# Last image's z by channel chunk, each chunk normalized in one operation per tile and written for all images while the next chunk is made

## Chip, cores, metric

One core of one Trainium2 chip. The time is the device time of that core in microseconds (us), the median of several executions; lower is better.

## What is computed

Eight images of 512 channels and 32 x 32 positions, fp32, pass two layers. The first is attention with 8 heads and a residual. The second is a non-local block whose last steps matter here:

```python
f_div_C = einsum('bcn,bdn->bcd', theta_x, phi_x) / n
y = einsum('bcd,bdn->bcn', f_div_C, g_x)
z = conv1x1(y, W_w, W_b) + x
mean = z.mean(axis=(0, 2, 3)); var = z.var(axis=(0, 2, 3))      # over all images
out = (z - mean) * rsqrt(var + 1e-5) * gamma + beta
```

Mean and variance run over all images and positions of a channel. So no output of a channel can be written before z of the *last* image is known for that channel, but different channels don't wait for each other.

## The kernel before

Channels lie on 128 partitions in four chunks (`CC` = 4). z of images 0 to 5 is spilled to HBM, images 6 and 7 stay in SBUF (`KEEP` = 2). During the last image, images 0 to 2 are reloaded into buffers that fall free early; 3 to 5 follow at the end. `mats` holds the large matrices, `ring` has twelve blocks of 128x1024, and a pool's tag sets which tiles share a buffer.

```python
    # nonlocal_, for every image (cut): f from theta and phi, g, then wf = f * W
        nc.scalar.copy(wf, ps)
        ...                                  # eight sums on VectorE for the seven-product form
        seven(f"pz_{b}", Blocks(), data, False, first_z, add_to(xt))     # x += wf * g, all chunks
        for oc in range(CC):
            for h in range(NH):
                nc.vector.bn_stats(stats[:, oc, b * NH + h, :], xt[:, oc, h * 512:(h + 1) * 512])
            ...                              # spill of images 0 to 5
    # after the last image
    reload(3, "o")                           # buffer of theta and phi of the last image
    for b in range(4, B - KEEP):
        reload_chunks(b)                     # images 4 and 5, into ring blocks
    ...                                      # a soundness count is loaded into registers
    for cc in range(CC):
        nc.vector.bn_aggr(mv[:, cc, :], stats[:, cc, :, :].rearrange("p s k -> p (s k)"))
    ...                                      # gs = gamma / sqrt(var + eps) for all chunks
    for b in sorted(z, reverse=True):
        for cc in range(CC):
            t = z[b][cc]
            nc.vector.tensor_scalar(t, t, mv[:, cc, 0:1], gs[:, cc:cc + 1], ALU.subtract, ALU.mult)
            nc.scalar.activation(t, t, AF.Identity, bias=beta[:, cc:cc + 1])
            nc.sync.dma_start(out_v[b, :, cc, :], t)
```

`seven` is a seven-product (Strassen-like) form of a 2x2 block matrix product. All transfers named here are issued by SP (SyncE).

## Time and profile before

| | before |
|---|---|
| time, median of the first 3 runs | 2346.35 us (2342.19 to 2347.3) |
| span of the profiled run, granted clock | 2342.2 us, 0.982 |
| TensorE busy | 2240.7 us, 96% |
| gap between last reads and first writes | 11.2 us |
| writes of the output | 41.6 us at 402 GB/s |

Two terms of the profile: the *share* is the mean busy share of the core's 16 DMA engines, which do the transfers, and the *granted clock* is the part of full speed that TensorE's clock ran at.

The profile is read from the end of the span backwards, because only the end is touched: first the slices, then windows of the last 70 us, then the timeline. Those lines stand in the prediction. One more line is needed as a mark. The copy of f on ScalarE ends the part that the change does not reach; its timeline line in the kernel before is

```profile
2269.23 0.60 ACT L361 ACTIVATE f<-pf 128x512 f32<-128x512 f32 x1 [11.37 <-PE pf L359]
```

(columns: start in us, duration, engine, line, operation, output<-input, shapes, count, and in brackets the engine's idle time before it and who ended it). **f to end** below means the span's end less the start of this line: 2342.2 - 2269.23 = 73.0 us here. It is the measure of most experiments, because the 2270 us before f vary from run to run.

### The profile page before, as it was taken

Reading aid. Unit: us, or ns where it says so; the run is one execution under the profiler, and the core shown is the slowest. Engines: PE = TensorE matmul, PEld = TensorE weight load, DVE = VectorE, ACT = ScalarE, POOL = GpSimd, SP = SyncE. Lnnn points to the kernel's source line nnn. Section 1 sums busy time; section 2 is a strip of 40 time slices with the busy share of each in tenths; the row PEclk is TensorE's granted clock in tenths of the full one; section 3 lists DMA queues with packets and bytes.
Section 4 is the critical chain, followed back from the end, with each engine's and each line's share of the span. In section 5 each row is a group of like instructions: output and inputs, shape, how many; then the busy total and the mean of one; then the engine's idle time right before and its main releaser. Section 6 shows DMA issues by size and latency. Waiting matters only on the chain.

```text
span 2342.2 us, 20797 instructions
## 1 busy us (share of the span) xinstructions
PE 2240.7 (96%) x8562; PEld 1127.6 (48%) x8562; DVE 1397.7 (60%) x1261; ACT 704.4 (30%) x819; POOL 61.7 (3%) x56
## 2 busy tenths in 40 slices
PE   4999999999999999999999999999999999999990
PEld 1533655336643466434563355633655346643360
DVE  2277445783567744687348854488445773477745
ACT  0155102541035310453104521154202541035205
POOL 2000110000000000000000000000000000000000
PEclk7999999999999999999999999999999999999995
DMA  6000122001130021200121002210113001200327
GB/s 233 1 1 7 64 85 108 28 1 63 47 135 1 1 76 66 104 1 32 48 94 72 1 32 76 90 48 1 63 47 135 1 1 63 79 16 1 108 86 310
DMA packets 30950, 141.94 MB, mean 61 GB/s; under 512 B 4096, under 2 KB 10496, under 8 KB 26112
## 3 DMA queue, kind: packets, MB, share of 16 engines
q1 hardware_dynamic: 26000, 131.87, 15.2%
q10 hardware_dynamic: 4848, 8.67, 1.0%
q8 instruction: 69, 1.13, 0.2%
q14 instruction: 33, 0.27, 0.0%
HBM read 101.07 MB, written 39.45 MB: 60 GB/s over the span
## 4 chain that ended last, share of the span: by engine, by line
PE 94%; ACT 2%; DVE 1%; DMA 1%; POOL 0%; issue 0%; ACTq 0%; DVEq 0%; POOLq 0%
PE ps L270 20%; PE po L289 17%; PE pv L171 8%; PE ptp L171 8%; PE pk L171 8%; PE pp L171 8%; PE pq L171 8%; PE pg L171 4%; PE pz L171 4%; PE pf L359 2%; PE psum L289 1%; PE pwf L378 1%; ACT z L504 1%; PE po L287 1%; PE po L286 1%; PE psum L287 1%
## 5 line engine op out<-in xcount | busy, mean ns | idle before, releaser
L273 ACT ACTIVATE e<-ps 128x1024 f32<-128x1024 f32 x512 | 482.5, 1030 | 360.3 <-PE ps L270 360.3
L279 DVE TENSOR_TENSOR acc<-acc,e 128x1024 f32<-128x1024 f32 x384 | 467.4, 1217 | 164.0 <-ACT e L273 135.7
L270 PE MATMUL ps<-q,k 64*128 64x512 f32 x2048 | 473.3, 603 | 1.6 <-POOL q L256 1.6
L289 PE MATMUL po<-e,v 128*64 128x512 f32 x1904 | 464.3, 594 | 0.0
L270 PEld LDWEIGHTS ps<-q,k 64*128 64x128 f32 x2048 | 187.6, 187 | 284.2 <-issue 233.6
L289 PEld LDWEIGHTS po<-e,v 128*64 128x64 f32 x1904 | 153.3, 137 | 211.9 <-issue 200.7
L297 DVE RECIPROCAL ri<-psum 128x512 f32<-128x512 f32 x64 | 214.5, 3352 | 10.2 <-PE psum L289 10.2
L368 ACT ACTIVATE g<-pg,gb 128x512 f32<-128x512 f32 x32 | 22.0, 687 | 428.6 <-PE pg L171 428.6
L171 PE MATMUL pq<-t_x,w_WqT 128*128 128x512 f32 x256 | 117.8, 608 | 26.0 <-ACT q L228 21.1
L188 DVE TENSOR_TENSOR k<-k,pk 128x1024 f32<-128x1024 f32 x24 | 29.3, 1221 | 163.1 <-PE pk L171 163.1
L171 PE MATMUL pp<-t_o,w_WpT 128*128 128x512 f32 x256 | 116.3, 602 | 1.9 <-DVE x L331 1.9
L171 PE MATMUL ptp<-w_tp,t_x 128*128 128x256 f32 x512 | 114.4, 379 | 0.0
L171 PE MATMUL pv<-w_WvT,t_x 128*128 128x256 f32 x512 | 114.4, 379 | 0.0
L171 PE MATMUL pk<-t_x,w_WkT 128*128 128x512 f32 x256 | 113.8, 592 | 0.0
L171 PEld LDWEIGHTS ptp<-w_tp,t_x 128*128 128x128 f32 x512 | 97.3, 190 | 13.2
L171 PEld LDWEIGHTS pv<-w_WvT,t_x 128*128 128x128 f32 x512 | 97.3, 190 | 13.2
L228 ACT ACTIVATE q<-pq,bq 128x512 f32<-128x512 f32 x64 | 40.4, 684 | 182.8 <-PE pq L171 182.8
L171 PE MATMUL pq<-x,w_WqT 128*128 128x512 f32 x192 | 88.7, 605 | 5.3 <-DMA w_WqT<-in_WqT_dram 5.3
L171 PEld LDWEIGHTS pq<-t_x,w_WqT 128*128 128x128 f32 x256 | 49.9, 196 | 90.1 <-issue 62.4
L188 DVE TENSOR_TENSOR q<-q,pq 128x1024 f32<-128x1024 f32 x24 | 29.3, 1221 | 102.1 <-PE pq L171 102.1
L277 DVE TENSOR_TENSOR acc<-e,e 128x1024 f32<-128x1024 f32 x64 | 78.3, 1223 | 16.6 <-ACT e L273 15.7
L171 PE MATMUL pp<-o,w_WpT 128*128 128x512 f32 x192 | 88.2, 603 | 0.0
(117 smaller groups left out, 2193.2 us busy)
## 6 DMA issues: line engine op xcount, KB each, us to landing
x<-in_x_dram SPq DMA_DIRECT2D x32, 512.0 KB, 5.5
w_WpT<-kept_WpT SPq DMA_DIRECT2D x7, 1792.0 KB, 7.1
w_tp<-kept_tp SPq DMA_DIRECT2D x7, 1792.0 KB, 7.2
spill<-x SPq DMA_DIRECT2D x24, 512.0 KB, 3.8
z<-spill SPq DMA_DIRECT2D x24, 512.0 KB, 8.4
out_dram<-z SPq DMA_DIRECT2D x24, 512.0 KB, 6.0
w_WqT<-kept_WqT SPq DMA_DIRECT2D x6, 1792.0 KB, 7.4
w_WvT<-kept_WvT SPq DMA_DIRECT2D x6, 1792.0 KB, 7.0
```

What stands on the lines that cost most here:

```text
L171: pe(nc.tensor.matmul(to_ps, lhsT(k), rhs(k), start=(s, at) not in begun, stop=(k == nk - 1), skip_group_check=True))
L188: nc.vector.tensor_tensor(at, at, ps, ALU.add)
L228: nc.scalar.activation(t[:, c, cols(q)], ps[:, m, :], AF.Identity, bias=bias[:, c:c + 1])
L270: pe(nc.tensor.matmul(ps[:, j, :], k[r, p, m * P:(m + 1) * P], q[r, p, h * 512:(h + 1) * 512], start=True, stop=True))
L273: nc.scalar.activation(e, ps, AF.Exp, scale=SCALE)
L277: nc.vector.tensor_tensor(accs[p, h], es[p, h, 0], e, ALU.add)
L279: nc.vector.tensor_tensor(accs[p, h], accs[p, h], e, ALU.add)
L286: pe(nc.tensor.matmul(to[:, :LEAD], l, r[:, :LEAD], start=start, stop=False, skip_group_check=True))
L287: pe(nc.tensor.matmul(to[:, LEAD:], l, r[:, LEAD:], start=False, stop=stop, skip_group_check=True))
L289: pe(nc.tensor.matmul(to, l, r, start=start, stop=stop, skip_group_check=True))
L297: nc.vector.reciprocal(ri, ps)
L359: pe(nc.tensor.matmul(ps[:, c, :], tp[:, i, c * P:(c + 1) * P], tp[:, i, CI:], start=(i == 0), stop=(i == NB - 1)))
```

## The change

Intent: start writing as soon as the first chunk of channels is done. For the last image z is made chunk by chunk with a plain product; each chunk is then aggregated, and each of its eight tiles (one per image) is normalized in *one* operation, `t * gs + (beta - mean * gs)`, alternately on VectorE and ScalarE, and written while TensorE and VectorE make the next chunk.

```diff
+        if before_z:
+            before_z()                       # reloads of images 3, 4, 5
+            last_z(b, xt, wf, g)
+            return
...
+    def last_z(b, xt, wf, g):
+        z[b] = [xt[:, oc, :] for oc in range(CC)]
+        for oc in range(CC):
+            ps = next_bank(f"pz_{b}_{oc}")
+            for h in range(NH):
+                s = slice(h * 512, (h + 1) * 512)
+                for d in range(IC):
+                    pe(nc.tensor.matmul(ps[:, h, :], wf[:, d, oc * P:(oc + 1) * P], g[d][:, s], ...))
+                nc.vector.scalar_tensor_tensor(xt[:, oc, s], ps[:, h, :], wb[:, oc:oc + 1], xt[:, oc, s],
+                                               ALU.add, ALU.add)
+                nc.vector.bn_stats(stats[:, oc, b * NH + h, :], xt[:, oc, s])
+            batch_norm(oc)
+
+    def batch_norm(oc):
+        nc.vector.bn_aggr(mv[:, oc, :], ...)
+        nc.scalar.activation(gs, mv[:, oc, 1:2], AF.Sqrt, bias=eps)
+        ...                                  # gs = gamma / that; shift = beta - mean * gs
+        for i, b in enumerate(sorted(z, reverse=True)):
+            t = z[b][oc]
+            if i % 2:
+                nc.scalar.activation(t, t, AF.Identity, bias=shift, scale=gs)
+            else:
+                nc.vector.tensor_scalar(t, t, gs, shift, ALU.mult, ALU.add)
+            nc.sync.dma_start(out_v[b, :, oc, :], t)
...
-    (the reloads after the last image, the aggregation of all chunks,
-     and the loop over images with two operations per tile)
```

More of the change, by code (lines that the diff above doesn't have):

```diff
@@ L212, in unshifted @@
         nc.vector.memset(heads[j * D:(j + 1) * D, j * D:(j + 1) * D], 1.0)
+    mv = const.tile([P, CC, 2], F32, tag="mv", name="mv")
     gates = const.tile([P, B * NPAIR], F32, tag="gates", name="gates")
@@ L349, in theta_phi, with nonlocal_ @@
         return tp
-    def nonlocal_(b, xt, data, tp, wg):
+    def nonlocal_(b, xt, data, tp, wg, before_z):
         g = [w2.tile([P, N], F32, tag="acc", name=f"g_{b}_{d}") for d in range(IC)]
@@ L373, in nonlocal_ @@
         wf = block(f"wf_{b}")
-        ws = block(f"ws_{b}")
         ps = next_bank(f"pwf_{b}")
@@ L380, in nonlocal_ @@
         nc.scalar.copy(wf, ps)
+        if before_z:
+            before_z()
+            last_z(b, xt, wf, g)
+            return
         half = C // 2
+        ws = block(f"ws_{b}")
         w = [wf[:, 0, :half], wf[:, 1, :half], wf[:, 1, half:]] + [ws[:, i, j * half:(j + 1) * half]
@@ L413, in nonlocal_ @@
                 nc.sync.dma_start(spill[b][:, oc, :], xt[:, oc, :])
+    def last_z(b, xt, wf, g):
[5 more added lines that the diff above has]
+                for d in range(IC):
+                    pe(nc.tensor.matmul(ps[:, h, :], wf[:, d, oc * P:(oc + 1) * P], g[d][:, s],
+                                        start=(d == 0), stop=(d == IC - 1)))
+                nc.vector.scalar_tensor_tensor(xt[:, oc, s], ps[:, h, :], wb[:, oc:oc + 1], xt[:, oc, s],
[3 more added lines that the diff above has]
+    def batch_norm(oc):
+        nc.vector.bn_aggr(mv[:, oc, :], stats[:, oc, :, :].rearrange("p s k -> p (s k)"))
+        gs, shift = (small.tile([P, 1], F32, tag=n, name=f"{n}_{oc}") for n in ("gs", "shift"))
+        nc.scalar.activation(gs, mv[:, oc, 1:2], AF.Sqrt, bias=eps)
+        nc.vector.reciprocal(gs, gs)
+        nc.vector.tensor_tensor(gs, gs, gamma[:, oc:oc + 1], ALU.mult)
+        nc.vector.tensor_tensor(shift, mv[:, oc, 0:1], gs, ALU.mult)
+        nc.vector.tensor_tensor(shift, beta[:, oc:oc + 1], shift, ALU.subtract)
+        for i, b in enumerate(sorted(z, reverse=True)):
[5 more added lines that the diff above has]
+            nc.sync.dma_start(out_v[b, :, oc, :], t)
     z = {}
@@ L428, in reload_chunks, with reload_rest @@
             z[b].append(t)
+    def reload_rest():
+        reload(3, "o")
+        for b in range(4, B - KEEP):
+            reload_chunks(b)
     data = data_sums(quarters_of(xt), "x_0")
@@ L470, in unshifted @@
             w["v"] = load_w("WvT", b + 2, nc.sync, None)
-        nonlocal_(b, xt, data, tp, w["g"])
+        nonlocal_(b, xt, data, tp, w["g"], reload_rest if last else None)
         if b < B - 2:
             w["k"] = load_w("WkT", b + 2, nc.sync, None)
-        if b >= B - KEEP:
+        if B - KEEP <= b < B - 1:
             z[b] = [xt[:, cc, :] for cc in range(CC)]
         xt = nxt.get("x")
-    reload(3, "o")
-    for b in range(4, B - KEEP):
-        reload_chunks(b)
     good = const.tile([P, 1], F32, tag="good", name="good")
@@ L488, in unshifted @@
     sound = nc.values_load(count, min_val=0, max_val=P)
-    mv = const.tile([P, CC, 2], F32, tag="mv", name="mv")
-    for cc in range(CC):
-        nc.vector.bn_aggr(mv[:, cc, :], stats[:, cc, :, :].rearrange("p s k -> p (s k)"))
-    rstd = const.tile([P, CC], F32, tag="rstd", name="rstd")
-    nc.scalar.activation(rstd, mv[:, :, 1], AF.Sqrt, bias=eps)
-    nc.vector.reciprocal(rstd, rstd)
-    gs = const.tile([P, CC], F32, tag="gs", name="gs")
-    nc.vector.tensor_tensor(gs, rstd, gamma, ALU.mult)
-    for b in sorted(z, reverse=True):
-        for cc in range(CC):
-            t = z[b][cc]
-            nc.vector.tensor_scalar(t, t, mv[:, cc, 0:1], gs[:, cc:cc + 1], ALU.subtract, ALU.mult)
-            nc.scalar.activation(t, t, AF.Identity, bias=beta[:, cc:cc + 1])
-            nc.sync.dma_start(out_v[b, :, cc, :], t)
     return sound
```

## The prediction

> **What bounds the kernel now.** Read first the page's rows by slices, then the chain, then the windows of the last 70 us, because the change touches only the last image's z and what follows it: with line numbers and buffer numbers taken off, the instruction order of both kernels is the same on every engine up to the product that makes the last z.
>
> ```profile
> PE   4999999999999999999999999999999999999990
> DMA  6000122001130021200121002210113001200327
> PE 94%; ACT 2%; DVE 1%; DMA 1%; POOL 0%; issue 0%; ACTq 0%; DVEq 0%; POOLq 0%
> ```
>
> TensorE is busy in all but the first and last slice of 58.6 us each, and the chain is 94% TensorE. So some 2275 of 2342 us are closed to this change. The last slice alone has an idle TensorE and a DMA row at 7. Cut finely, that end is three stretches and a rest (columns: stretch, length, busy time of PE, PEld, DVE, ACT, POOL, granted clock, DMA share, GB/s):
>
> ```profile
> 2270.40:2286.70 16.30, 15.14 (x36) 6.21 (x35) 10.21 (x16) 2.98 (x3) 0.00 (x0) 1.00 0.99 378
> 2286.90:2297.10 10.20, 1.20 (x5) 0.35 (x3) 9.77 (x19) 1.49 (x3) 0.00 (x0) 0.74 0.02 6
> 2298.00:2339.60 41.60, 0.00 (x0) 0.00 (x0) 20.29 (x29) 31.29 (x31) 0.00 (x0) 0.50 1.01 402
> 2339.70:2342.20 2.50, 0.00 (x0) 0.00 (x0) 0.00 (x0) 0.00 (x0) 0.00 (x0) 0.50 0.04 16
> ```
>
> First the transfers read spilled z back at a full DMA share (0.99). Then for some 11 us they do nothing (0.02) while VectorE finishes the last z, its statistics and the mean and variance. Then the 32 writes of the output run at share 1.01 and 402 GB/s until 2339.6. In that third stretch ScalarE is busy 31.3 of 41.6 us and VectorE 20.3, so neither holds the writes back: the end is set by the DMA engines. The chain view names ACT there ("ACT z L504"), since it follows instructions; it stops at 2329.3, 10 us before the last byte. The timeline around the gap:
>
> ```profile
> 2271.07 6.65 SPq L427 DMA_DIRECT2D z<-spill  x8
> ...
> 2275.50 1.98 PE L171 MATMUL pz<-g,wf 128*128 128x512 f32 x4 [1.16 <-ACT wf L380]
> ...
> 2292.38 1.91 DVE L493 BATCH_NORM_AGGREGATE mv<-stats 128x2 f32<-128x96 f32 x4
> ...
> 2295.06 5.87 DVE L503 TENSOR_SCALAR x<-x,mv,gs 128x1024 f32<-128x1024 f32 x8
> ...
> 2297.08 8.26 SPq L505 DMA_DIRECT2D out_dram<-x  x8
> ```
>
> The last z starts at 2275.5; the first write can go only after all four channel chunks have z, statistics and scale, at 2297.1. The reads ended at about 2286.8. The gap is 2298.0 - 2286.8 = **11.2 us**.
>
> **What the Trainium skill says.** (1) "DMA: Bandwidth & Descriptors", section "Queues, rings and completion order": on each DMA engine the descriptors of one ring are consumed in ring order. Reads and writes are all issued by SP, so early writes queue up behind the reads and don't overtake them. The trace agrees: the reloads at L427 took 7.8 to 10.9 us to land, where eight transfers of 1.3 us (0.524 MB at 402 GB/s) stand in line. (2) The same page, "Where 436 GB/s comes from", lets the HBM side bind at about 358 GB/s. The trace differs: 402 GB/s over 41.6 us of writes. I use 402. (3) "ScalarE: Activation LUTs", "What ACT_TABLE_LOAD costs": about 280 ns + 0.833 ns per element with one per-partition pointer operand, 93 ns more for each further one. The trace agrees for one: 280 + 853 = 1133 ns, and L504 has 1134. The new form takes bias and scale by pointer: an estimate from that section of 1.23 us. (4) "VectorE: DVE Perf Modes", "Mode 2×_2P": fp32 tensor_scalar from SBUF to SBUF may take two elements a cycle, tensor_tensor can't. The trace agrees: 0.82 us for L503 against 1.21 for L188 on the same 128x1024. The new tensor_scalar with two pointers is the same form as L503, so it stays fast.
>
> ```profile
> L504 ACT ACTIVATE z<-z,beta 128x1024 f32<-128x1024 f32 x24 | 25.1, 1134 | 0.0
> L503 DVE TENSOR_SCALAR z<-z,mv,gs 128x1024 f32<-128x1024 f32 x24 | 17.5, 825 | 0.0
> L404 DVE SCALAR_TENSOR_TENSOR x<-pz,Wb,x 128x512 f32<-128x512 f32 x8 | 5.6, 744 | 0.7 <-PE pz L171 0.7
> L411 DVE BATCH_NORM_STATS2 stats<-x 128x6 f32<-128x512 f32 x8 | 5.1, 680 | 0.0
> L493 DVE BATCH_NORM_AGGREGATE mv<-stats 128x2 f32<-128x96 f32 x4 | 1.9, 530 | 0.0
> ```
>
> **The change, part by part.** *The product.* The seven-product form is left for the last image: 14 matmuls become 16 plain ones. A matmul shows as two records 0.43 us apart, so 32 x 0.43 = 13.8 us in place of 28 x 0.43 = 12.0: 1.8 us more TensorE. A chunk is four matmuls, 3.4 us. It starts as before, when wf is copied (2275.5). Gone from VectorE are eight small sums for that form (4 x 0.69 + 4 x 0.42 = 4.4 us) and three additions of 1.21.
>
> *The first write.* TensorE gives the first half of chunk 0 at 2277.3 and the second at 2279.0. VectorE adds the second half to x (0.7, to 2279.8), takes its statistics (0.7, to 2280.5), aggregates (0.5, to 2281.0). ScalarE's square root takes 0.3, but in the compiled order VectorE puts an addition and statistics of chunk 1 in between (1.4, to 2282.4). Then the reciprocal (0.18) and three one-column operations of 0.16, with gaps 0.8, to 2283.2; one tensor_scalar, 0.8, to **2284.0**. Before, it was 2297.1: 13.1 us earlier. It is also 2.8 us before the reads end, so the DMA engines should not fall idle: before, data moved some 0.9 us after the first issue, which gives 2284.9 against 2286.8.
>
> *Feeding it.* A chunk is written for all 8 images: 8 x 0.524 MB = 4.19 MB, 10.4 us at 402 GB/s. VectorE needs per chunk 2 x 0.70 (add) + 2 x 0.61 (statistics, back to back) + 0.46 + 0.18 + 3 x 0.16 + 4 x 0.73 (the spacing in L503's 24) = 6.7 us; ScalarE 0.3 + 4 x 1.13 to 1.23 = 4.8 to 5.2; TensorE 3.4. All lie under 10.4, beside the writes. The halving of ScalarE's normalizing (32 activations to 16, some 16 us less) is worth nothing, as it lay under the writes already.
>
> *The end.* Bytes are the same: 12 reloads and 32 writes. The writes start where the reads end: 2286.8 + 41.6 = 2328.4, plus the 2.5 us after the last byte = 2330.9 in place of 2342.2. The gain is the gap, **11.2 us**. One thing moves to the end: the load of the soundness count and the branch on it came before the writes in SP's order and now come after them. Before, the last issue was at about 2336 and the last byte at 2339.6, so some 3 us hide it; I add 0.2. Predicted: 2346.35 - 11.2 + 0.2 = **2335.4 us**.
>
> **Rivals.** *A new wait holds the first writes.* In the compiled order VectorE's first chunk is x of image 7, then images 3, 5 and 1. Image 5's chunk 0 is the ninth of twelve reloads and lands at about 2284, just when it is wanted; the writes stand in SP's order, so one late tile stops all behind it. If the first burst slips by 4 us, 1 to 2 us of the gap come back: 2337. Against it: four tiles are ready by 2286, 5 us of traffic. *Reads and writes that meet slow each other.* They meet only at the border, with up to eight transfers in line. If the meeting cost a tenth for 10 us, 1 us: 2336. The windows of before, where they don't meet, say nothing on it. *VectorE becomes the bound.* It would take over 10.4 us per chunk in place of 6.7; with waits for PSUM and for the square root I find no more than 8. If it did at 12, the writes would end some 6 us later: 2341. *The better side:* if the 13.1 us by which the first write is earlier were gained whole, 2333. Against it: the DMA engines were already full until 2286.8. *ScalarE sets the end*, as the chain suggests: then the earlier start (13 us) and the halved activations (16 us) would both count, some 29 us, 2317. Against it: the share of 1.01 and the ten microseconds of transfers after its last activation.
>
> **Range and chances.** Three runs of before spread over 5 us (2342 to 2347), which is half the gain, and another chip may add as much. The rivals reach from 2333 to 2341. So 2330 to 2341 for 8 in 10. A gain of 2% would be 47 us; the whole end from 2275.5 has 66.7, of which 41.6 are writes at full share, so it can't be had. Slower by 2% would need the writes to run at half their rate. Chances: faster 0.01, within 2% 0.985, slower 0.005.
>
> **What would show it right or wrong.** Right: the first write is issued near 2284; the DMA share stays near 1 from 2270.4 to about 2328 without a hole; the writes still run near 400 GB/s; VectorE is idle in between; the rest after the last byte is still about 2.5 us. Wrong: a hole in the DMA share after 2286.8 (late tiles or a long VectorE), a rate below 390 where reads and writes meet, a rest well above 2.5 us (the count and the branch), or ScalarE activations so long that writes wait for them.

## The result

The changed kernel took 2334.11 us (median of 6, 2331.6 to 2335.78), the kernel before 2343.26 (median of 6, 2341.89 to 2347.3). The ratio is 0.9957, 95% interval 0.9944 to 0.9970. Ratios here are the mean time of one kernel's fast runs over that of the other's of the same rounds, so they are not quite the ratio of the medians. The class is "same" at 2%, as forecast; the gain of some 10 us is outside the noise.

The slices of the changed kernel, on its page:

```profile
PE   4999999999999999999999999999999999999993
DMA  6000122001130012200112001210022001110309
```

The last DMA digit has gone from 7 to 9: the end is denser. Its windows (columns as in the prediction):

```profile
2269.10:2285.20 16.10, 13.02 (x30) 5.07 (x28) 7.19 (x14) 5.15 (x6) 0.00 (x0) 1.00 1.01 381
2285.20:2326.80 41.60, 7.82 (x16) 2.69 (x14) 19.85 (x40) 17.45 (x18) 0.00 (x0) 0.67 1.02 406
2326.90:2330.20 3.30, 0.00 (x0) 0.00 (x0) 0.00 (x0) 0.00 (x0) 0.00 (x0) 0.50 0.09 35
```

The stretch at share 0.02 is gone. Reads and writes now form one stream of 57.7 us at a full share, from 2269.1 to 2326.8. The writes' rate is 406 GB/s, so where reads and writes meet nothing is lost. The timeline of the first chunk (TensorE's weight loads left out):

```profile
2268.09 0.60 ACT L362 ACTIVATE f<-pf 128x512 f32<-128x512 f32 x1 [11.37 <-PE pf L360]
...
2274.36 1.99 PE L428 MATMUL pz<-g,wf 128*128 128x512 f32 x4 [1.16 <-ACT wf L380]
2276.39 0.75 DVE L430 SCALAR_TENSOR_TENSOR x<-pz,Wb,x 128x512 f32<-128x512 f32 x1 [14.51 <-PE pz L428]
...
2277.19 3.70 PE L428 MATMUL pz<-g,wf 128*128 128x512 f32 x8 [0.84 <-DVE x L430]
...
2280.73 0.59 DVE L437 BATCH_NORM_AGGREGATE mv<-stats 128x2 f32<-128x96 f32 x1
2281.23 0.68 DVE L430 SCALAR_TENSOR_TENSOR x<-pz,Wb,x 128x512 f32<-128x512 f32 x1
...
2281.95 0.69 DVE L432 BATCH_NORM_STATS2 stats<-x 128x6 f32<-128x512 f32 x1
...
2282.56 0.15 DVE L440 RECIPROCAL gs<-gs 128x1 f32<-128x1 f32 x1
...
2284.17 0.81 SPq L450 DMA_DIRECT2D out_dram<-x  x2
```

From f to the first write it is 16.1 us (before: 2297.08 - 2269.23 = 27.9), from f to the end 2330.2 - 2268.09 = **62.1 us** (before 73.0). The difference of 10.9 us is close to the predicted 11.0 (the gap of 11.2, less 0.2). Two delays ahead of the first write can be read here: TensorE stands 0.84 us before the second half of chunk 0 until VectorE has read the first, and VectorE does chunk 1's addition and statistics (0.68 and 0.69) before chunk 0's reciprocal. The groups from 2274 on:

```profile
L428 PE MATMUL pz<-g,wf 128*128 128x512 f32 x32 | 16.4, 655 | 9.3 <-DVE x L430 8.1 <-ACT wf L380 1.2
L447 ACT ACTIVATE z<-z,shift,gs 128x1024 f32<-128x1024 f32 x12 | 14.0, 1227 | 0.0
L449 DVE TENSOR_SCALAR z<-z,gs,shift 128x1024 f32<-128x1024 f32 x12 | 9.0, 808 | 0.0
```

ScalarE's activation with two per-partition operands takes 1227 ns (before, with one: 1134). TensorE waits 8.1 us for VectorE in this product, hidden under the writes.

### The profile page after: what moved, and what is told of

Its sections match the earlier page's. It is cut to its first block, busy times and chain, and to the rows that moved or that the text cites. A ratio compares the mean times of both kernels' runs of the same rounds, so it can differ in the third digit from the quotient of the medians.

```text
span 2330.2 us, 20778 instructions
## 1 busy us (share of the span) xinstructions
PE 2244.2 (96%) x8566; PEld 1128.4 (48%) x8566; DVE 1381.4 (59%) x1248; ACT 690.4 (30%) x806; POOL 61.9 (3%) x56
## 4 chain that ended last, share of the span: by engine, by line
PE 95%; DVE 2%; DMA 1%; ACT 1%; POOL 0%; issue 0%; ACTq 0%; DVEq 0%; POOLq 0%
PE ps L271 20%; PE po L290 17%; PE pv L171 8%; PE ptp L171 8%; PE pk L171 8%; PE pq L171 8%; PE pp L171 8%; PE pg L171 4%; PE pz L171 4%; PE pf L360 2%; PE psum L290 1%; PE pwf L378 1%; PE po L288 1%; PE po L287 1%; PE psum L288 1%; PE psum L287 1%
## 5 line engine op out<-in xcount | busy, mean ns | idle before, releaser
L188 DVE TENSOR_TENSOR k<-k,pk 128x1024 f32<-128x1024 f32 x24 | 29.3, 1221 | 163.1 <-PE pk L171 163.1
L188 DVE TENSOR_TENSOR q<-q,pq 128x1024 f32<-128x1024 f32 x24 | 29.3, 1221 | 102.5 <-PE pq L171 102.5
```

Of the source, the lines that this page charges most:

```text
L188: nc.vector.tensor_tensor(at, at, ps, ALU.add)
```

## The experiments

The theory: the transfers set the end, and the gain is the gap between reads and writes, closed by overlapping chunks. The rivals: fewer operations on ScalarE and VectorE gave it; or the plain product did. A later question was what holds the start of the writes now. Ratios are to the kernel before, of the same rounds. e1 to e4, e5 to e8, e9 and e10, and e11 ran on four different chips.

| run | ratio (95%) | f to first write | f to end |
|---|---|---|---|
| before | 1 | 27.9 | 73.0 |
| changed | 0.9957 (0.9944 to 0.9970) | 16.1 | 62.1 |
| changed, again (e5) | 0.9952 (0.9940 to 0.9965) | 16.1 | 61.9 |
| e1 two operations per tile | 0.9956 (0.9939 to 0.9973) | 16.9 | 62.5 |
| e2 one operation per tile, alone | 1.0002 (0.9985 to 1.0019) | 27.1 | 71.8 |
| e3 no overlap | 1.0004 (0.9987 to 1.0021) | 28.7 | 73.9 |
| e4 seven reads early | 0.9961 (0.9944 to 0.9977) | 16.1 | 61.5 |
| e6 first write sooner | 0.9950 (0.9937 to 0.9963) | 15.5 | 61.1 |
| e7 both | 0.9951 (0.9938 to 0.9963) | 15.5 | 60.8 |
| e8 and wf's first columns sooner | 0.9954 (0.9941 to 0.9967) | 14.8 | 60.2 |
| e9 and the halves in tiles of their own | one look | 13.5 | 58.9 |
| e9's kernel, timed (e11) | 0.9936 (0.9922 to 0.9950) | 13.5 | 58.8 |
| e10 half the writes (wrong) | one look | 16.1 | 46.0 |

All times in us. All results but e10's were correct.

### e1: the changed kernel with two operations per tile

```diff
-            if i % 2:
-                nc.scalar.activation(t, t, AF.Identity, bias=shift, scale=gs)
-            else:
-                nc.vector.tensor_scalar(t, t, gs, shift, ALU.mult, ALU.add)
+            nc.vector.tensor_scalar(t, t, mv[:, oc, 0:1], gs, ALU.subtract, ALU.mult)
+            nc.scalar.activation(t, t, AF.Identity, bias=beta[:, oc:oc + 1])
```

> The changed kernel with the old two operations per tile (a tensor_scalar on VectorE, then an activation on ScalarE), everything else as changed: undoes the 'one operation' part alone. Theory (the transfers set the end): per chunk VectorE needs about 9.2 us and ScalarE about 4.5, after which both still lie under the 10.4 us that a chunk's writes take (ScalarE 8 x 1.04 = 8.3); the first write goes one activation (1.1 us) later, which may open a hole of up to 1 us between reads and writes. So 0 to 1 us slower than the changed kernel (ratio to before 0.9957 to 0.9961), DMA share near 1 to the end. Rival (the gain came from ScalarE and VectorE doing less): 16 activations and 16 tensor_scalars come back, some 10 us or more slower, ratio to before near 1.000.

Ratio 0.9956, f to end 62.5: 0.4 to 0.7 us more than the changed kernel. Its windows:

```profile
2287.00:2297.00 10.00, 5.35 (x10) 2.03 (x8) 9.38 (x19) 8.65 (x10) 0.00 (x0) 0.83 1.00 395
2298.00:2329.00 31.00, 4.08 (x6) 1.46 (x6) 20.33 (x37) 23.23 (x24) 0.00 (x0) 0.58 1.02 404
```

ScalarE and VectorE are much busier (8.65 and 9.38 of the first 10 us), and the share stays at 1.00 and 1.02. The work that the single operation saves was hidden. The rival of fewer operations falls.

### e2: the kernel before with one operation per tile

```diff
-            nc.vector.tensor_scalar(t, t, mv[:, cc, 0:1], gs[:, cc:cc + 1], ALU.subtract, ALU.mult)
-            nc.scalar.activation(t, t, AF.Identity, bias=beta[:, cc:cc + 1])
+            if cc % 2:
+                nc.scalar.activation(t, t, AF.Identity, bias=shift[:, cc:cc + 1], scale=gs[:, cc:cc + 1])
+            else:
+                nc.vector.tensor_scalar(t, t, gs[:, cc:cc + 1], shift[:, cc:cc + 1], ALU.mult, ALU.add)
```

> The kernel before with one operation per tile (every second tile on ScalarE with scale and shift, the others on VectorE), still after all chunks: does the 'one operation' part alone. Theory: only the first write is sooner, by one activation less two small operations, about 0.8 us; ratio to before 0.9995 to 1.000. ScalarE's time in the write stretch falls from 33 to about 18 us without use. Rival (ScalarE set the end, as the chain of waits suggests): 10 us or more faster, ratio 0.995 or less.

Ratio 1.0002. The first write came 0.8 us sooner, and f to end fell from 73.0 to 71.8, 0.4 us more than the first write explains; what the rest is stays open. Its windows around the gap and of the writes:

```profile
2287.30:2296.50 9.20, 1.12 (x5) 0.27 (x3) 8.70 (x19) 1.02 (x2) 0.00 (x0) 0.77 0.01 4
2297.30:2338.90 41.60, 0.00 (x0) 0.00 (x0) 10.13 (x15) 16.69 (x15) 0.00 (x0) 0.50 1.02 404
```

The gap is there (share 0.01). ScalarE's part of the writes fell from 31.3 to 16.7 us, and the writes still take 41.6. The chain of waits, which named ScalarE at the end, was misleading.

### e3: the changed kernel without the overlap

```diff
                 nc.vector.bn_stats(stats[:, oc, b * NH + h, :], xt[:, oc, s])
-            batch_norm(oc)
+        for oc in range(CC):
+            batch_norm(oc)
```

VectorE's instructions of both functions were pinned to the program's order, since the scheduler otherwise mixes the chunks again.

> The changed kernel with all four chunks of z made first and only then statistics, scale and writes chunk by chunk (VectorE held to this order): undoes the overlap alone, and puts the load of the soundness count ahead of the writes again. Theory: the hole between reads and writes comes back, about 11 us, since the plain product with its waits takes some 18 us to the last chunk (4.6 us per chunk in the trace of the changed kernel); ratio to before 0.999 to 1.001. Rival (one operation per tile, or the simpler product, gave the gain): stays near 0.9957.

Ratio 1.0004: the gain is gone. The window of the gap:

```profile
2287.50:2298.50 11.00, 5.89 (x14) 2.31 (x14) 7.46 (x16) 1.24 (x2) 0.00 (x0) 1.00 0.01 2
```

Eleven microseconds at share 0.01 stand between reads and writes again, though the plain product and the single operation are both in. The overlap is the cause of the gain. The pinning is not what lost it: e6 pins VectorE too and keeps the gain. f to end is even 0.9 us longer than before, since the plain product gives its last chunk later: the last statistics end 26.2 us after f here and 23.2 us after f in the kernel before.

### e4: seven of the twelve last reads early

The twelve reads waited in SP's order behind the reload of image 3, whose buffer (theta and phi) falls free only at f. Seven of the eight blocks for images 4 and 5 are free much earlier.

```diff
         data = data_sums(quarters_of(xt), f"x1_{b}")
+        if last:
+            reload_chunks(4)
+            reload_chunks(5, 3)              # three of four chunks; the last one after image 3
```

> The changed kernel with seven of the twelve last reloads issued before the theta/phi product, where the ring has seven free blocks and the transfers are idle; five are left behind that product. Theory: in the changed kernel the reads ended at about 2285.2 and the first write was issued at 2284.2, so both hold the writes about equally: with 9 us fewer reads in front the writes start at most about 1 us sooner, and a hole of some 8 us opens between reads and writes. 0 to 1.5 us faster than the changed kernel, ratio to before 0.9951 to 0.9957. Rival (the reads in front alone hold the writes): 7 x 1.3 = 9 us faster, ratio 0.992.

f to end 61.5, 0.4 to 0.7 us less. The windows show where the 9 us of reads went:

```profile
2269.00:2276.00 7.00, 5.85 (x15) 2.29 (x13) 0.00 (x0) 2.98 (x3) 0.00 (x0) 1.00 0.99 348
2277.00:2284.00 7.00, 5.60 (x13) 2.38 (x14) 5.37 (x12) 0.83 (x2) 0.00 (x0) 1.00 0.00 1
2285.00:2326.00 41.00, 8.16 (x16) 2.70 (x14) 20.19 (x40) 17.79 (x18) 0.00 (x0) 0.68 1.02 403
```

They became a hole at share 0.00 before the first write, which didn't move. Fewer reads in front alone win little, so in the changed kernel the first write is nearly as late as the end of the reads; e6 tries the other half.

### e5 to e8: what holds the start of the writes

e5 is the changed kernel again, as the measure for another chip.

> The changed kernel again, as the measure for the three that follow on the same chip. Ratio to before near 0.9957, as measured first.

e6 has both halves of a chunk multiplied before VectorE's part, and VectorE pinned to the program's order:

```diff
             for h in range(NH):
                 ...matmuls of half h...
+            for h in range(NH):
                 nc.vector.scalar_tensor_tensor(...)      # pinned, and all of VectorE's in batch_norm
```

> The changed kernel with the first write made ready sooner: both halves of a chunk multiplied before VectorE reads the first (the trace showed the second half waiting 0.84 us for VectorE), and VectorE held to the order of the program, so that chunk 1's addition and statistics (1.4 us) do not come before chunk 0's scale. The first write should be issued about 2 us sooner, 14.1 us after the first of the last reloads in place of 16.1. The reads stay. Theory (reads and first write hold the writes about equally, since the reads end at the same time as the first write's data could go): 0 to 0.5 us faster than the changed kernel. Rival (the first write alone sets the start of the writes): 2 us faster.

e7 is e6 with the early reads of e4:

> Both together: seven reloads early, as in e4, and the first write about 2 us sooner, as in the run before. Neither alone should gain; together the start of the writes moves to the first write. Theory: about 2 us faster than the changed kernel, ratio to before about 0.9949, with the writes starting about 2 us sooner after the product of theta and phi. Rival (something else, such as the writes' own rate or the end of the program, sets the end): as the changed kernel.

e8 is e7 with `wf[:, :, :128]` copied first, by VectorE, into a tile of its own, while ScalarE copies the rest:

> As the run before, and the first 128 columns of wf copied on their own by VectorE, which stands idle then, beside ScalarE's copy of the rest, so that the last z starts about 0.6 us sooner. Theory: another 0.5 us, 2.5 us faster than the changed kernel, ratio to before about 0.9947. Rival: the smaller copy starts no sooner, or the later chunks fall behind and open a hole in the writes: as the run before or worse.

The times can't tell these apart (0.9950 to 0.9954, intervals of 0.0013 either way); f to end can: 61.9, 61.1, 60.8, 60.2. e6 gained 0.8 us where 0 to 0.5 was expected, and e7 only 1.1 where 2 was: the first write was 0.6 us sooner, not 2. Two profiles of the changed kernel differ by 0.2 us in f to end. e6's gain is not the earlier first write's. These are 17 us, almost all reads, and 38 us of writes after them (1 to 18 and 18 to 56 us after f), first in the changed kernel, then in e6:

```profile
2269.09:2286.09 17.00, 13.50 (x30) 5.07 (x28) 8.08 (x15) 6.04 (x7) 0.00 (x0) 1.00 1.01 383
2286.09:2324.09 38.00, 7.35 (x14) 2.69 (x14) 18.96 (x39) 16.56 (x17) 0.00 (x0) 0.68 1.02 408
2272.89:2289.89 17.00, 15.84 (x38) 6.80 (x37) 7.39 (x14) 6.65 (x7) 0.00 (x0) 1.00 1.00 383
2289.89:2327.89 38.00, 2.47 (x8) 0.91 (x6) 20.40 (x40) 16.06 (x17) 0.00 (x0) 0.56 1.03 415
```

The reads move as before, without a hole after them; the writes ran at 415 GB/s in place of 408 (407 in e5). Over some 41 us that is 0.7 us. Why they did is open; e7, with the same instructions in this part, has 405. So in the changed kernel an earlier first write alone wins nothing that can be seen. e7's shortfall has a cause in its timeline:

```profile
2274.32 14.00 PE L428 MATMUL pz<-g,wf 128*128 128x512 f32 x32 [1.15 <-ACT wf L380]
2278.06 0.75 DVE L432 SCALAR_TENSOR_TENSOR x<-pz,Wb,x 128x512 f32<-128x512 f32 x1 [16.21 <-PE pz L428]
```

TensorE now runs through, but VectorE begins 3.7 us after it, when *both* halves are multiplied. In the changed kernel it began after 2.0. Both halves lie in one tile of PSUM, the memory that TensorE writes its products to. The first read seems to wait for the last write to that tile: what TensorE no longer waited, VectorE did. e9 tests this.

### e9 and e11: the halves in tiles of their own

```diff
+            if oc:
+                half = [ps[:, h, :] for h in range(NH)]
+            else:
+                half = [psO.tile([P, 512], F32, tag="o", name=f"pz_{b}_{oc}_{h}") for h in range(NH)]
```

> As e8, with the two halves of chunk 0 in two PSUM tiles of their own. In e6, e7 and e8 the multiplies ran through without a pause, but VectorE began only when both halves were done (3.7 us after the first multiply), so the first write came only 0.6 us sooner in place of 2. Theory (the wait belongs to the shared PSUM tile): VectorE takes the first half's addition and statistics (1.4 us) while the second half is multiplied; first write 13.4 to 13.6 us after f in place of 14.8, time from f to the end 58.8 to 59.2 us in place of 60.2. Rival (VectorE waits for something else): no change.

```profile
2267.00 0.60 ACT L362 ACTIVATE f<-pf 128x512 f32<-128x512 f32 x1 [11.37 <-PE pf L360]
...
2272.63 14.00 PE L435 MATMUL pz<-g,wf 128*128 128x512 f32 x32 [0.52 <-DVE wf L382]
...
2274.65 0.75 DVE L439 SCALAR_TENSOR_TENSOR x<-pz,Wb,x 128x512 f32<-128x512 f32 x1 [2.08 <-PE pz L435]
...
2280.45 0.81 SPq L459 DMA_DIRECT2D out_dram<-x  x2
```

VectorE begins 2.0 us after TensorE, TensorE still runs through, the first write comes 13.45 us after f and the end 58.9: as expected, and the wait was the shared tile's. With the reads early, the end follows the first write: from e4 over e7 and e8 to e9 the first write came 2.6 us sooner (16.06 to 13.45 after f), and so did the end (61.46 to 58.90). The same kernel timed in five rounds:

> The kernel of e9 again, now timed in five rounds against the kernel before. From f to the end it took 58.9 us, 14.1 us less than the kernel before (73.0) and 3.1 less than the changed kernel (62.0); so ratio to before 0.9935 to 0.9945, where the changed kernel had 0.9952 to 0.9957. If the part before f got longer through the earlier reads, the ratio stays above 0.995.

2329.81 us (2327.51 to 2333.16) against 2343.0; ratio 0.9936, 0.9922 to 0.9950. By f to end it beats the changed kernel by 3.0 to 3.4 us and is the best version found; the intervals of the ratios (0.9922 to 0.9950 and 0.9940 to 0.9965) still overlap a little.

### e10: half the writes

```diff
-            nc.sync.dma_start(out_v[b, :, oc, :], t)
+            if b >= B // 2:
+                nc.sync.dma_start(out_v[b, :, oc, :], t)
```

> The changed kernel with the writes of images 0 to 3 left out, so that its result is wrong on purpose: measures what the writes cost by themselves. All arithmetic stays. Theory (the transfers set the end): 16 of 32 writes at 1.3 us fall away, 20.8 us; but VectorE and ScalarE finish the last chunk some 38 us after f, and 5 to 6 us pass from there to the end, so the time from f to the end falls from 62 to 42 to 44 us. Rival (VectorE, ScalarE or the end of the program sets the end): 55 us or more.

f to end fell from 62.0 to 46.0, by 16.0 us: a little less than expected, far from the rival's 55. Two windows say why not the whole 20.8:

```profile
2295.00:2300.00 5.00, 0.80 (x2) 0.50 (x2) 4.94 (x9) 4.78 (x5) 0.00 (x0) 0.77 0.56 222
2312.00:2314.00 2.00, 0.00 (x0) 0.00 (x0) 0.00 (x0) 0.00 (x0) 0.00 (x0) 0.50 1.01 389
```

With half the writes the share falls to 0.56 while VectorE and ScalarE are busy all the time (4.94 and 4.78 of 5 us): in that stretch the arithmetic has become the bound. With all the writes it is not.

## Why the prediction was right

- **Total.** Predicted 2335.4 in 2330 to 2341; measured 2334.11. The predicted gain was 11.0 us; f to end gives 10.9, the ratio 10.1 (0.0043 x 2343.26), the medians 9.2. The median of before itself moved by 3.1 us between three and six runs, so the closeness of the absolute number is partly luck. So is that of the gain: the full stretch ended 58.7 us after f in place of 70.4, 11.7 us sooner and so more than the gap, and the rest after it grew by 0.8 (below), so that two misses cancel.
- **What sets the end**, the transfers: shown by e1 (more arithmetic, at most 0.7 us longer), e2 (less arithmetic, 1.2 us shorter, of which the first write explains 0.8) and e10 (fewer writes, 16 us shorter). With this the rival that ScalarE sets the end fell.
- **The gain is the gap**: shown by e3, where the gap comes back and the gain goes.
- **First write.** Predicted at 2284.0 and seen at 2284.17, but f was 1.1 us sooner in that run: counted from f, 14.8 was predicted and 16.1 measured. The step that failed is "TensorE gives the first half of chunk 0 at 2277.3 and the second at 2279.0": it took no account of TensorE waiting 0.84 us for VectorE between the halves. VectorE began the second half 4.9 us after the product's start, where the prediction had 3.5; the steps from there to the first write took the 5.0 us that were predicted. Of the 1.4 us, 0.84 are that wait; the rest is not broken down. It cost nothing measurable, because the reads ended only then; e4 and e6 show how close it was.
- **Feeding.** VectorE's 6.7 us per chunk: the first normalizations of the four chunks start at 2283.33, 2291.96, 2297.15 and 2303.29, on average 6.65 apart, though not evenly (8.6, 5.2, 6.1).
- **The two-operand operations.** ScalarE's activation was estimated at 1.23 us and measured at 1.227; VectorE's tensor_scalar was to stay at 0.82 and took 0.808. The prediction compared the latter with L188, which reads one operand from PSUM; L279 (acc<-acc,e), with both in SBUF, took 1.217, so the comparison stands.
- **The rest after the last byte.** Predicted 2.5 + 0.2; the window after 2326.9 is 3.3 us at share 0.09, with a trickle of transfers in it (before: 2.5 us at share 0.04). This term was too small, and "a rest well above 2.5 us" was named as a sign of being wrong. The count is not the cause: SP loads it from 2323.8 to 2325.2, the last write lands at 2328.8, and from that landing to the end it is 1.39 us in both kernels. e3, which loads the count before the writes, has 3.1 us too (2340.5 to 2343.6). Why the trickle is longer stays open.
- **The rivals.** Late tiles, a slow meeting of reads and writes (406 GB/s) and VectorE as the bound did not come. "If the 13.1 us ... were gained whole" did not come either: the reads were in front, as argued, and e4 shows that without them the first write is.

## What to carry to other kernels

When an end consists of reads, a reduction and writes, look at the share of the transfers in fine windows before counting operations: an idle stretch between two full ones is what an overlap can win, and arithmetic saved under a full stretch is worth nothing. The chain of waits names the last instructions, not the transfers that outlast them. Once a stream is gapless, two things can hold its start together (here the reads in front and the first result), so move both, and look for waits that belong to a shared buffer rather than to the data.

## What the Trainium skill lacked or had wrong

- "DMA: Bandwidth & Descriptors", section "Where 436 GB/s comes from", says that HBM binds transfers between HBM and SBUF at about 358 GB/s. In this program on one core the writes ran at 402 to 406 GB/s for 41.6 us at a share of 1.01 to 1.02. The same section also names a measured 425 GB/s, so the page has a case above 358 itself; what the rule of 358 lacks there is when it holds.
- "PSUM — Partial Sum Buffer", section "PSUM bank collisions raise a hardware error", advises guarding PSUM by bank and quadrant. The kernel's semaphores guard more: a tile of 128x2x512 fp32 values, 4 KiB per partition and so two of that page's 2 KiB banks, was waited for as a whole. No page gives the price of this. Here splitting the tile (e9) brought the first write from 14.8 to 13.5 us after f, with a correct result; the 0.84 us that TensorE waited in the changed kernel fit the same cause, but no run tests them alone.
- No page has the times of VectorE's batch norm instructions. Here the statistics of 128x512 took 0.69 us and the aggregation of 128x96 0.53 to 0.59 us.
